# Splitting the first batch pair of a hybrid block into two units, and moving token weighting and softplus sums from VectorE to GpSimd

## The chip, the cores and the metric

The kernel runs on one NeuronCore of a Trainium2 chip. TensorE (PE) multiplies matrices into PSUM, VectorE (DVE) and ScalarE (ACT) do elementwise work, GpSimd (POOL) does some elementwise work and issues DMAs, and the queue of SyncE (SP) issues DMAs. Each engine runs its own list of instructions in order, and semaphores order the engines against each other. The metric is the device time of one execution in microseconds (us); lower is better.

## The reference

The input is 8 batches of 256 tokens with 128 features, in fp32. Four residual layers follow each other:

```
x = x + mamba(layernorm(x))     # selective state space, 256 channels, 16 states
x = x + moe(layernorm(x))       # 8 experts, top 2, inner width 352
x = x + gated_attention(layernorm(x))   # relu(scores)**2
x = x + moe(layernorm(x))       # the same expert weights
```

In the first layer each channel i and state n runs a recurrence over the tokens, `new = exp(A[i,n] * d_t) * state + d_t * B_t[n] * h_t`, and its output sums `new * C_t[n]` over the 16 states and adds `D * h_t`. Here `d = softplus(ts @ dt_w + dt_b)`, and `h` is a causal convolution of width 4 followed by silu. The expert layer gives every token a weight for each expert (zero outside its two best) and adds `w_e * ((x @ w_up) * silu(x @ w_gate)) @ w_down` over the experts.

## The kernel before, in words

The eight batches are four groups of two (`SIZES`, L133), so a group is 512 tokens, and most tiles are 128 features by 512 tokens. Five kinds of work exist for a group g:

- `prelude(g)` (lane s, L518): layer norm, projection, convolution (by DVE for groups 0 and 3, by PE for groups 1 and 2, `CONV`), then B, C and the softplus. B and C go to DRAM as `bc`. The softplus is `max(z,0) + ln(1 + exp(-|z|))` with a correction for the rounding of `1 + exp`. Its four elementwise steps, L622 (the correction), L624 (`dl -= ex`), L632 (`dl += ww`) and L633 (`du = dl * h`), are DVE instructions.
- `recurrence(g)` (lane m, L724): sixteen steps, one for each pair of a chunk of states and a half of the channels. A step is three DVE instructions on a 128x1024 tile `st`: L744 (`st = bt * du`), the scan L749, and L753 (`st *= ct`). A lane of its own (`feeder`, L666) has SP load `bt` and `ct`, broadcast from DRAM, and has ACT make `decay` by exponentials (L697). A tile holds `CHUNK // GB` = 2 states of 512 tokens. Another lane (`adder`, L709) sums the `st` tiles over the chunks by accumulating DMAs on POOL's queue (L716).
- `gating(g)` (lane g) and `ending(g)` (lane f): for groups 0 and 1 PE sums what is left of the states with the identity as weights (tile `y`); the product with the gate is L797 or L784.
- `tail(g)` (lane t): the projection back (`pb_m`), added to the residual x by L512.
- `rest(g)` (lane r): expert layer `p`, attention `a`, expert layer `r`, then the store. An expert layer is `led_in` (norm, router, ranks, weights `we`) and `moe` (22 blocks of gate `gp`, ScalarE's silu `sg`, up `up`, DVE's product `it` at L1000, and down `dn`). The up product of an expert takes tokens already multiplied by their weight: `wb` is loaded by a broadcast DMA on ACT's queue (L969) and multiplied by `xT` on DVE (`weighted`, L974, L977). For the layers in `SOON` the product of expert 0 is made in `led_in` (L940).

All groups run interleaved. The order on every engine is fixed when the program is built, by a planner (`Board`, L32): each lane offers its next operation with an estimated duration, the planner computes when it could start from what it believes of the engines, buffers and inputs, takes the engine that could start first, and among the lanes ready there within a lane's patience the one of lowest rank (`RANKS`). A switch of ScalarE's function table adds 1.3 us to an estimate (`SWITCH`). Where the planner sees PE idle ahead of a product, it fills the time with products of the identity into the same bank (`fill` in `pe`, L320 to L327); in the profile these stand under L325, with two records for each fp32 product. They compute nothing.

The estimates are written beside each operation: `dve_us(512)` is 0.69 us, and the planner knows nothing of one engine slowing another.

Of the kernel before, what the change touches and what calls it, by code (L numbers as in the profile page):

```python
# [31 lines left out]
class Board:  # L32
# [4 lines left out]
    PATIENCE, LONG = 0, 0  # L37
# [58 lines left out]
def kernel(  # L96
# [28 lines left out]
    P = 128  # L125
# [25 lines left out]
        "s": [0, 4, 4, 1.5], "m": [1.5, 2, 3, 3.5],  # L151
        "g": [4, 0, 3.5, 2], "t": [0, 3.5, 3.5, 0.5],
        "r": [2, 0.5, 2.5, 0.5], "f": [2.5, 1.5, 4, 0.5], "w": [0, 0, 0.3, 0], "feeder": 5, "adder": 0,
    }
    SOON = ("p0", "p1", "r0", "p3", "r3")
    SPLIT = ()
# [125 lines left out]
    def ring(pool, shape, tag, name, bufs=1):  # L282

        held = rings.setdefault((pool.name, tag), [])
        free = held[-bufs].used if len(held) >= bufs else 0.0
        h = Held(pool.tile(shape, FP, tag=tag, name=name, bufs=bufs), free)
        held.append(h)
        return h
# [51 lines left out]

    def mm(n):
        return 0.005 + 0.00167 * n
# [37 lines left out]
    ]  # L380
    xh = [
# [4 lines left out]
    padding = [Held(t) for t in padded]  # L386
# [131 lines left out]
    def prelude(g):  # L518

        GB = SIZES[g]  # L520
        G = GB * T
        xn = yield from layernorm(Held(xs[g]), f"m{g}", "m", rms=True, parts=xh[g])
        for held in xh[g]:
            yield from biased(held, b_first)
        xT = ring(norm, [P, G], "xTm", f"xT_m{g}")
        yield from transposed(xn, f"m{g}", xT, scale=col("norm_scale"))
# [3 lines left out]
        h = [ring(mam, [P, G], f"h{c}", f"h_{g}_{c}", bufs=2) for c in range(NI)]  # L530
        cv = ring(mam, [P, NI, GB, T], "ex", f"cv_{g}")
        for c in range(NI):
            hp = padding[c]
            ps = bank([P, G], f"hid_{g}_{c}")
            yield pe(mm(G), [ps], [xT], product(ps.ap, [(in_w_sb[:, c * P : (c + 1) * P], xT.ap)]))
            yield act(act_us(G), [hp], [ps], lambda: nc.scalar.activation(
                hp.ap[:, 0:GB, K - 1 :], ps.ap.rearrange("p (b t) -> p b t", b=GB),
# [4 lines left out]
            if g in CONV:  # L542
                cps = bank([P, GB, T], f"conv_{g}_{c}")
                yield pe(K * mm(G), [cps], [hp], product(
                    cps.ap, [(taps_sb[:, k, c, :], hp.ap[:, 0:GB, k : k + T]) for k in range(K)]
                ))
                yield act(act_us(G), [h[c]], [cps], lambda: nc.scalar.activation(
                    h[c].ap.rearrange("p (b t) -> p b t", b=GB), cps.ap, AF.Silu,
                    bias=col("conv_b", c),
                ), SILU)  # L550
                shut(cps)
                continue

            if g > 0:
                yield act(act_us(G), [cv], [hp], lambda: nc.scalar.mul(
                    cv.ap[:, c], hp.ap[:, 0:GB, 0:T], col("conv_w", c)
                ))

            def taps():
                if g == 0:  # L560
                    nc.vector.tensor_scalar_mul(cv.ap[:, c], hp.ap[:, 0:GB, 0:T], col("conv_w", c))
                for k in range(1, K):
                    nc.vector.scalar_tensor_tensor(
                        cv.ap[:, c], hp.ap[:, 0:GB, k : k + T], col("conv_w", k * NI + c),
                        cv.ap[:, c], ALU.mult, ALU.add,
                    )

            yield dve((K - (g > 0)) * dve_us(G), [cv], [hp], taps)
        for c in range(0 if g in CONV else NI):
            yield act(act_us(G), [h[c]], [cv], lambda: nc.scalar.activation(  # L570
                h[c].ap, cv.ap[:, c].rearrange("p b t -> p (b t)"), AF.Silu, bias=col("conv_b", c)
# [3 lines left out]
        ps = bank([P, G], f"xpj_{g}")  # L575
# [4 lines left out]
        ww = ring(mam, [P, NI, G], "ww", f"ww_{g}")  # L580
# [3 lines left out]
        bc = Held(dram.tile([2 * N, G], FP, tag="bc", name=f"bc_{g}"))  # L584
# [4 lines left out]
        dl = [ring(mam, [P, G], f"dl{c}", f"dl_{g}_{c}", bufs=2) for c in range(NI)]  # L589
        ex = ring(mam, [P, NI, G], "ex", f"ex_{g}")  # L590
        for c in range(NI):
            ps = bank([P, G], f"dt_{g}_{c}")
# [19 lines left out]
        du = [ring(mam, [P, G], f"du{c}", f"du_{g}_{c}", bufs=2) for c in range(NI)]  # L612
# [6 lines left out]
        for (a, b), e, w in zip(parts, exs, wws):  # L619

            def lost():
                nc.vector.scalar_tensor_tensor(e.ap, w.ap, 1.0, e.ap, ALU.subtract, ALU.subtract)  # L622
                for c in range(a, b):
                    nc.vector.tensor_sub(dl[c].ap, dl[c].ap, e.ap[:, c - a, :])  # L624

            yield dve(2 * (b - a) * dve_us(G), [e] + dl[a:b], [w], lost)
        for (a, b), w in zip(parts, wws):
            yield act(act_us((b - a) * G), [w], [], lambda: nc.scalar.activation(w.ap, w.ap, AF.Ln, bias=zero), EXP)
        for (a, b), w in zip(parts, wws):
            for c in range(a, b):  # L630
                def step():
                    nc.vector.tensor_add(dl[c].ap, dl[c].ap, w.ap[:, c - a, :])  # L632
                    nc.vector.tensor_mul(du[c].ap, dl[c].ap, h[c].ap)  # L633

                yield dve(2 * dve_us(G), [dl[c], du[c]], [w, h[c]], step)
# [6 lines left out]
        led_up[g] = bc, h, xT, dl, du  # L642

    def gating(g):

        xT = led_up[g][2]
        G = SIZES[g] * T
        gate = [ring(mam, [P, G], f"g{c}", f"g_{g}_{c}") for c in range(NI)]
        for c in range(NI):
            ps = bank([P, G], f"gat_{g}_{c}")  # L650
# [6 lines left out]
        gates[g] = gate  # L657
# [8 lines left out]
    def feeder():  # L666

        for g in range(NG):
            while f"s{g}" not in done:
                yield None  # L670
            GB = SIZES[g]
            G = GB * T
            NC = CHUNK // GB
            bc, h, _, delta, du = led_up[g]
            for q in range(N // NC):
# [4 lines left out]
                for tag, r0 in (("bt", q * NC), ("ct", N + q * NC)):  # L680
                    t = ring(scan, [P, NC, G], tag, f"{tag}_{g}_{q}", bufs=2)
# [5 lines left out]
                fed[g, q] = *rows_at, das  # L687
                for c in range(NI):
# [15 lines left out]
                    yield act(0.81 * NC, [da], [delta[c]], issue, EXP)  # L704
# [4 lines left out]
    def adder():  # L709

        while len(done & {f"f{g}" for g in range(NG)}) < NG:
# [3 lines left out]
            g, us, acc, st, into, of = sums.pop(0)  # L715
# [4 lines left out]
            landed[g] = landed.get(g, 0) + 1  # L720
# [3 lines left out]
    def recurrence(g):  # L724
        GB = SIZES[g]
# [3 lines left out]
        bc, h, _, delta, du = led_up[g]  # L729
# [4 lines left out]
        for q in range(NQ):  # L734
            for c in range(NI):
                while not spare():
                    yield None
                st = state([P, NC, G], f"st_{g}_{q}_{c}")
                if q == 0:
                    acc.append(st)  # L740
                while len(fed.get((g, q), [[]])[-1]) <= c:
                    yield None
                bt, ct, das = fed[g, q]
# [13 lines left out]
                elif q > 0:  # L757
                    sums.append((g, 6.3, acc[c], st, acc[c].ap, st.ap))
                    count[c] += 1
                elif g > 0:  # L760

                    sums.append((g, 4.5, acc[c], h[c], acc[c].ap[:, 0, :], h[c].ap))
                    count[c] += 1
        recurred[g] = acc, last, sum(count)
# [5 lines left out]
    def ending(g):  # L770

        G = SIZES[g] * T
        NC = CHUNK // SIZES[g]
        acc, last, count = recurred.pop(g)
        bc, h, _, delta, du = led_up[g]
        if g in FOLD:
            for c in range(NI):
                sums.append((g, 4.5, acc[c], acc[c], acc[c].ap[:, 0, :], acc[c].ap[:, 1, :]))
                count += 1
        while landed.get(g, 0) < count or g not in gates:  # L780
            yield None
        for c in range(NI):
            if g in FOLD:
                yield dve(dve_us(G), [du[c]], [gates[g][c], acc[c]], lambda: nc.vector.tensor_mul(  # L784
                    du[c].ap, acc[c].ap[:, 0, :], gates[g][c].ap
# [3 lines left out]
            y = bank([P, G], f"y_{g}_{c}")  # L789
# [7 lines left out]
            yield dve(dve_us(G), [du[c]], [gates[g][c], y], lambda: nc.vector.tensor_mul(  # L797
                du[c].ap, y.ap, gates[g][c].ap
# [3 lines left out]
    def tail(g):  # L802
        gates.pop(g)
        bc, h, _, delta, du = led_up.pop(g)
        G = SIZES[g] * T
        yield from forked((RANKS["t"][g], g), [
            project_back(
                xh[g][p], of_part(g, p, du), out_w_sb, f"m{g}{p}"
            ) for p in range(len(PARTS[g]))
        ])  # L810
# [134 lines left out]
    def moe(g, which, key, shared, ends):  # L945
# [28 lines left out]
        def weighted(e):  # L974

            wb = wx[e]
# [334 lines left out]
```

## Time and profile before

| What | Value |
|---|---|
| Median of 3 runs | 759.33 us (759.11 to 759.85) |
| The profiled execution: its time / its span | 758.34 us / 756.6 us |
| PE busy | 737.7 us (98%) |
| DVE busy | 568.6 us (75%) |
| ACT busy | 431.1 us (57%) |
| POOL busy | 89.8 us (12%) |
| Scans (L749), count and mean | 64, 2309 ns |
| Products `wb * xT` (L977), count | 59 |
| Accumulating DMAs on POOL's queue (L716) | 64 |

The span runs from the first instruction's start to the last one's end; the time of the execution has 1.74 us around it. A busy PE is not a PE that does useful work here, since the filling products count as busy.

### The profile page before, as it was taken

The numbers are of one execution on the slowest core, as the hardware profiler recorded it, in microseconds if no ns is written. First come the engines' busy times: TensorE is split into PE (matmuls) and PEld (weight loads), VectorE is DVE, ScalarE is ACT, GpSimd is POOL, SyncE is SP. The second block draws the span as 40 slices with busy tenths as digits, with TensorE's granted clock in tenths as the row PEclk, the third lists the DMA queues.
The fourth block names the chain that finished last, engine by engine and source line by source line (L and its number), as shares of the span: only waits on it lengthen the run. The fifth ranks groups of instructions, "written<-read, shape, count | busy, mean of one in ns | idle before, by whom it ended". The sixth has DMA issues, their size and how long they took to land.

```text
span 756.6 us, 8464 instructions
## 1 busy us (share of the span) xinstructions
PE 737.7 (98%) x3093; PEld 403.6 (53%) x3093; DVE 568.6 (75%) x824; ACT 431.1 (57%) x570; POOL 89.8 (12%) x110
## 2 busy tenths in 40 slices
PE   4999999999999999999999999999999999999997
PEld 3877996853446744434754533443555434644343
DVE  2599999999999999899999998995735334354332
ACT  5578333799947879977876677742252322432220
POOL 2021110311112210002120110011100001000000
PEclk9999999999999999999999999999999999999999
DMA  8719795399763345655774666745011200000110
GB/s 260 209 57 220 169 219 162 98 228 218 166 171 84 76 124 133 166 133 138 176 170 96 159 161 179 160 102 109 2 42 27 72 15 14 15 29 29 47 36 14
DMA packets 38903, 88.63 MB, mean 117 GB/s; under 512 B 4339, under 2 KB 14542, under 8 KB 38862
## 3 DMA queue, kind: packets, MB, share of 16 engines
q0 software_dynamic: 9312, 30.94, 22.8%
q1 hardware_dynamic: 20624, 41.54, 17.2%
q10 hardware_dynamic: 8926, 15.61, 6.8%
q8 instruction: 24, 0.39, 0.2%
q14 instruction: 17, 0.14, 0.0%
HBM read 55.71 MB, written 1.44 MB: 76 GB/s over the span
## 4 chain that ended last, share of the span: by engine, by line
PE 78%; DVE 15%; ACT 3%; issue 2%; ACTq 0%; DVEq 0%
PE gp_r L487 10%; PE dn_r L1006 10%; PE dn_p L1006 9%; PE gp_p L487 9%; PE up_r L986 7%; PE up_p L986 7%; DVE st L749 6%; PE up_r L993 3%; DVE st L744 3%; PE up_p L993 3%; DVE st L753 2%; PE av_a L1197 2%; PE tp_p L325 1%; PE xpj L325 1%; PE v_a L1131 1%
## 5 line engine op out<-in xcount | busy, mean ns | idle before, releaser
L749 DVE TENSOR_TENSOR_SCAN st<-decay,st 128x1024 f32<-128x1024 f32 x64 | 147.8, 2309 | 2.5
L960 ACT ACTIVATE sg_r<-gp_r,zero 128x512 f32<-128x512 f32 x88 | 59.9, 687 | 109.8 <-PE gp_r L487 88.7
L57 ACT ACT_TABLE_LOAD x89 | 114.2, 1283 | 8.0 <-PE dn_r L1006 3.6
L697 ACT ACTIVATE decay<-dl,zero,a_sb 128x510 f32<-128x510 f32 x128 | 96.2, 804 | 36.9 <-DVE st L749 35.7
L1000 DVE TENSOR_TENSOR it_r<-up_r,sg_r 128x512 f32<-128x512 f32 x88 | 60.4, 687 | 66.7 <-PE up_r L986 42.3
L960 ACT ACTIVATE sg_p<-gp_p,zero 128x512 f32<-128x512 f32 x88 | 59.3, 685 | 62.5 <-PE gp_p L487 46.6
L1000 DVE TENSOR_TENSOR it_p<-up_p,sg_p 128x512 f32<-128x512 f32 x88 | 60.3, 686 | 43.4 <-PE up_p L986 29.4
L1006 PE MATMUL dn_p<-it_p,wd_sb 128*128 128x512 f32 x176 | 91.2, 605 | 0.6 <-DVE it_p L1000 0.6
L1006 PE MATMUL dn_r<-it_r,wd_sb 128*128 128x512 f32 x176 | 90.5, 603 | 0.0
L716 POOL DMA_DIRECT2D st<-st x58 | 50.4, 874 | 334.2 <-DVE st L753 303.7
L487 PE MATMUL gp_r<-xT_r,wg_sb 128*128 128x512 f32 x176 | 90.0, 597 | 0.0
L487 PE MATMUL gp_p<-xT_p,wg_sb 128*128 128x512 f32 x176 | 89.0, 594 | 0.0
L744 DVE TENSOR_TENSOR st<-bt,du 128x1024 f32<-128x1024 f32 x64 | 78.8, 1231 | 0.0
L753 DVE TENSOR_TENSOR st<-st,ct 128x1024 f32<-128x1024 f32 x64 | 78.1, 1221 | 0.7
L986 PE MATMUL up_p<-wb_p,wu_sb 128*128 128x512 f32 x128 | 65.1, 594 | 0.0
L986 PE MATMUL up_r<-wb_r,wu_sb 128*128 128x512 f32 x128 | 64.9, 592 | 0.0
L1006 PEld LDWEIGHTS dn_p<-it_p,wd_sb 128*128 128x128 f32 x176 | 31.3, 189 | 47.1 <-issue 36.3
L487 PEld LDWEIGHTS gp_r<-xT_r,wg_sb 128*128 128x128 f32 x176 | 32.6, 190 | 42.7 <-issue 37.4
L1006 PEld LDWEIGHTS dn_r<-it_r,wd_sb 128*128 128x128 f32 x176 | 31.6, 190 | 44.3 <-issue 39.5
L487 PEld LDWEIGHTS gp_p<-xT_p,wg_sb 128*128 128x128 f32 x176 | 32.8, 190 | 41.2 <-issue 36.3
L325 PEld LDWEIGHTS y<-ident 128*128 128x128 f32 x428 | 48.0, 192 | 1.2 <-PE dt L487 0.8
L325 PE MATMUL y<-ident 128*128 128x128 f32 x428 | 48.2, 275 | 0.0
(217 smaller groups left out, 853.1 us busy)
## 6 DMA issues: line engine op xcount, KB each, us to landing
st<-st POOLq DMA_DIRECT2D x54, 512.0 KB, 6.4
bt<-bc SPq DMA_DIRECT2D x32, 512.0 KB, 6.0
ct<-bc SPq DMA_DIRECT2D x32, 512.0 KB, 4.5
wb_r<-wrow_r ACTq DMA_DIRECT2D x30, 256.0 KB, 3.8
wb_p<-wrow_p ACTq DMA_DIRECT2D x29, 256.0 KB, 3.9
st<-h POOLq DMA_DIRECT2D x6, 256.0 KB, 4.9
wg_sb<-in_L_ffn_w_gate_dram SPq DMA_DIRECT2D x2, 704.0 KB, 4.7
wu_sb<-in_L_ffn_w_up_dram SPq DMA_DIRECT2D x2, 704.0 KB
```

What stands on the lines that cost most here:

```text
L57: self.load_tables(op.table)
L325: nc.tensor.matmul(ps[:, 0:n], lhsT=ident[:, 0:m], rhs=ident[:, 0:n], start=True, stop=True)
L487: nc.tensor.matmul(ps, lhsT=lhsT, rhs=rhs, start=(i == 0), stop=(i == len(terms) - 1))
L697: nc.scalar.activation(shaped[:, n, :, 1:], delta[c].ap.rearrange("p (b t) -> p b t", b=GB)[:, :, 1:], AF.Exp, bias=zero, scale=a_sb[:, c, ...
L716: yield load(us, [acc], [st], lambda: nc.gpsimd.dma_start(into, of, accum_op=ALU.add), "POOL", 0.9)
L744: yield dve(1.22, [st], [bt, du[c]], lambda: nc.vector.tensor_mul(st.ap, bt.ap, du[c].ap.unsqueeze(1).to_broadcast([P, NC, G])))
L749: yield dve(2.29, [st], [das[c]], lambda: nc.vector.tensor_tensor_scan(flat, das[c].ap.rearrange("p n t -> p (n t)"), flat, 0.0, ALU.mult, ...
L753: yield dve(1.22, [st], [ct], lambda: nc.vector.tensor_mul(st.ap, st.ap, ct.ap))
L960: yield act(act_us(G), [sg], [gp], lambda: nc.scalar.activation(sg.ap, gp.ap, AF.Silu, bias=zero), SILU)
L986: nc.tensor.matmul(ps.ap, lhsT=wu_sb[:, i * P : (i + 1) * P], rhs=wa.ap[:, cols_of], start=True, stop=True,)
L1000: yield dve(dve_us(width), [it], [ps, sg], lambda: nc.vector.tensor_mul(it.ap, ps.ap, sg.ap[:, cols_of]))
L1006: yield pe(mm(dn.ap.shape[1]), [dn], [it], lambda: nc.tensor.matmul(dn.ap, lhsT=wd_sb[:, i, :], rhs=it.ap[:, cols_of], start=(i == 0), sto ...
```

## The change

The change does four things.

1. `SPLIT = (0,)`: the two batches of group 0 become units of their own for everything up to the first expert layer. `UNITS` is now a list of five (group, first batch, last batch), and prelude, gating, recurrence, ending and tail take a unit. The two units share tiles of the group's size (`room`), each using its 256 columns. A recurrence chunk of such a unit has `CHUNK // 1` = 4 states of 256 tokens, so a unit has eight steps and the group still has sixteen, on tiles of the same 128x1024. `led_in` of the first expert layer runs for each unit as soon as its tail is done (`come`); after both, the group is one part again and `moe` runs on 512 tokens as before.
2. For the layers `p0`, `r0`, `p1`, `r1` and `p2`, `weighted` issues the product `wb * xT` on POOL (the program has 37 of them there, and 22 are left on DVE).
3. For groups 1 to 3 the softplus' `dl -= ex` and `dl += ww` go to POOL: four instructions of 128x512 in each group, twelve in all. Group 0 keeps them on DVE.
4. The planner's ranks are other ones, the second unit's prelude has a rank made worse by 1.5, and `LONG` is 0.2 instead of 0. The order on every engine changes with that.

```diff
-    PATIENCE, LONG = 0, 0
+    PATIENCE, LONG = 0, 0.2
...
-        "s": [0, 4, 4, 1.5], "m": [1.5, 2, 3, 3.5],
-        "g": [4, 0, 3.5, 2], "t": [0, 3.5, 3.5, 0.5],
-        "r": [2, 0.5, 2.5, 0.5], "f": [2.5, 1.5, 4, 0.5], "w": [0, 0, 0.3, 0], "feeder": 5, "adder": 0,
+        "s": [1.5, 2, 4, 0.5], "m": [1.5, 2, 3, 2.5],
+        "g": [4, 3.5, 2.5, 0.5], "t": [0, 3.5, 1, 3.5],
+        "r": [2, 0.5, 1, 0.5], "f": [2.5, 0, 3.5, 0.5], "w": [0.6, 0.6, 0.3, 0], "late": 1.5, "feeder": 2.5, "adder": 0,
     }
     SOON = ("p0", "p1", "r0", "p3", "r3")
-    SPLIT = ()
+
+    SPARED = ("p0", "r0", "p1", "r1", "p2")
+    SPLIT = (0,)
...
+    def room(pool, u, tag, name, both=False, bufs=1):
+
+        g, lo, hi = UNITS[u]
+        if (g, tag, name) not in rooms:
+            shape = [P, NI, SIZES[g] * T] if both else [P, SIZES[g] * T]
+            rooms[g, tag, name] = ring(pool, shape, tag, f"{name}_{g}", bufs)
+            rooms[g, tag, name].views = []
+        t = rooms[g, tag, name]
+        ap = t.ap[:, :, lo * T : hi * T] if both else t.ap[:, lo * T : hi * T]
+        h = Held(ap, t.used)
+        t.views.append(h)
+        return h
...
+    def pool_us(n):
+        return 0.1 + 0.0024 * n
...
+    UNITS = [(g, lo, hi) for g in range(NG) for lo, hi in PARTS[g]]
+    UNITS_OF = [[u for u, unit in enumerate(UNITS) if unit[0] == g] for g in range(NG)]
...
-    def prelude(g):
-
-        GB = SIZES[g]
+    def prelude(u):
+
+        g, lo, hi = UNITS[u]
+        GB = hi - lo
...
-                nc.vector.scalar_tensor_tensor(e.ap, w.ap, 1.0, e.ap, ALU.subtract, ALU.subtract)
-                for c in range(a, b):
-                    nc.vector.tensor_sub(dl[c].ap, dl[c].ap, e.ap[:, c - a, :])
-
-            yield dve(2 * (b - a) * dve_us(G), [e] + dl[a:b], [w], lost)
+
+            yield dve(dve_us((b - a) * G), [e], [w], lost)
+            for c in range(a, b):
+                if g > 0:
+                    yield pool(pool_us(G), [dl[c]], [e], lambda: nc.gpsimd.tensor_tensor(
+                        dl[c].ap, dl[c].ap, e.ap[:, c - a, :], ALU.subtract
+                    ))
+                else:
+                    yield dve(dve_us(G), [dl[c]], [e], lambda: nc.vector.tensor_sub(
+                        dl[c].ap, dl[c].ap, e.ap[:, c - a, :]
+                    ))
...
-                def step():
-                    nc.vector.tensor_add(dl[c].ap, dl[c].ap, w.ap[:, c - a, :])
-                    nc.vector.tensor_mul(du[c].ap, dl[c].ap, h[c].ap)
-
-                yield dve(2 * dve_us(G), [dl[c], du[c]], [w, h[c]], step)
+                if g > 0:
+                    yield pool(pool_us(G), [dl[c]], [w], lambda: nc.gpsimd.tensor_tensor(
+                        dl[c].ap, dl[c].ap, w.ap[:, c - a, :], ALU.add
+                    ))
+                else:
+                    yield dve(dve_us(G), [dl[c]], [w], lambda: nc.vector.tensor_add(
+                        dl[c].ap, dl[c].ap, w.ap[:, c - a, :]
+                    ))
+                yield dve(dve_us(G), [du[c]], [dl[c], h[c]], lambda: nc.vector.tensor_mul(
+                    du[c].ap, dl[c].ap, h[c].ap
+                ))
...
-                    yield act(0.81 * NC, [da], [delta[c]], issue, EXP)
+                    yield act((0.35 + 0.0009 * G) * NC, [da], [delta[c]], issue, EXP)
...
         def weighted(e):
 
             wb = wx[e]
+            if nm in SPARED:
+                yield pool(pool_us(G), [wb], [xT], lambda: nc.gpsimd.tensor_tensor(
+                    wb.ap, wb.ap, xT.ap, ALU.mult
+                ))
+                return
             yield dve(dve_us(G), [wb], [xT], lambda: nc.vector.tensor_mul(wb.ap, wb.ap, xT.ap))
...
-        yield from forked((RANKS["r"][g], g), [led_in(g, "p", key, p, first) for p in parts])
+        def come(p):
+            while f"t{UNITS_OF[g][p]}" not in done:
+                yield None
+            yield from led_in(g, "p", key, p, first)
+
+        yield from forked((RANKS["r"][g], g), [come(p) for p in parts])
+        if len(parts) > 1:
+
+            joined = Held(xs[g])
+            joined.ready = max(h.ready for h in xh[g])
+            joined.used = max(h.used for h in xh[g])
+            PARTS[g][:], xh[g][:] = [(0, SIZES[g])], [joined]
...
+    def lane(kind, n, g, work, after):
+
+        late = RANKS["late"] if kind == "s" and n in UNITS_OF[g][1:] else 0
+        waiting.append(Lane((RANKS[kind][g] + late, n), work, after))
...
+    for u, (g, lo, hi) in enumerate(UNITS):
+        prior = [v for v in UNITS_OF[g - 1]] if g > 0 else []
+        older = [v for v in UNITS_OF[g - 2]] if g > 1 else []
+        lane("s", u, g, prelude(u), [f"g{v}" for v in prior] + [f"t{v}" for v in older])
+        lane("m", u, g, recurrence(u), [f"s{u}"] + [f"m{u - 1}"] * (u > 0))
+        lane("g", u, g, gating(u), [f"s{u}"] + [f"t{v}" for v in prior])
+        lane("f", u, g, ending(u), [f"m{u}"])
+        lane("t", u, g, tail(u), [f"f{u}", f"g{u}"] + [f"t{u - 1}"] * (u > 0))
+        if lo == 0:
+            lane("r", g, g, rest(g), [f"t{u}"] + [f"r{g - 2}"] * (g > 1))
```

How the two programs differ in numbers of instructions, read from the programs themselves:

| Instruction | Before | After |
|---|---|---|
| PE: filling products of the identity | 564 | 462 |
| of these, ahead of the first gate product of layer `p0` | 430 | 345 |
| PE: `y` products | 14 of 512 columns | 4 of 512 and 36 of 256 |
| DVE, all | 824 | 812 |
| POOL: elementwise 128x512 products and sums that were on DVE | 0 | 49 |
| POOL: accumulating DMAs | 64 | 60 |
| ACT: `decay` exponentials | 128 of 510 columns | 96 of 510 and 64 of 255 |
| ACT: table loads | 89 | 93 |
| SP: writes of `bc` / loads of `bt` and `ct` | 4 / 64 | 5 / 64 |

## Prediction, made before the changed kernel ran

> **What bounds the kernel now.** I read the page's busy times first, then the engines by stretch of time, then who makes DVE wait, and last the chain of work that ended last. The columns of the second table are stretch, its length, then busy time and instructions of each engine, granted clock, DMA share and GB/s.
>
> ```profile
> PE 737.7 (98%) x3093; PEld 403.6 (53%) x3093; DVE 568.6 (75%) x824; ACT 431.1 (57%) x570; POOL 89.8 (12%) x110
> L325 PE MATMUL y<-ident 128*128 128x128 f32 x428 | 48.2, 275 | 0.0
> ```
>
> ```profile
> 41.00:158.00 117.00, 115.27 (x803) 95.07 (x802) 114.47 (x111) 66.34 (x89) 21.50 (x22) 1.00 0.66 160
> 158.00:511.00 353.00, 351.81 (x1278) 171.74 (x1277) 330.75 (x441) 269.36 (x335) 51.64 (x54) 1.00 0.62 149
> 511.00:530.00 19.00, 19.00 (x60) 7.77 (x59) 10.48 (x14) 4.72 (x7) 2.61 (x3) 1.00 0.52 105
> 530.00:756.60 226.60, 221.47 (x760) 104.38 (x758) 95.33 (x214) 66.88 (x103) 7.62 (x7) 1.00 0.10 29
> ```
>
> ```profile
> DVE it_p L1000 <- PE up_p L986: 7.7, 13, 1.7
> DVE it_r L1000 <- PE up_r L986: 4.2, 6, 1.1
> DVE it_r L1000 <- PE up_r L993: 1.1, 3, 0.7
> DVE x L479 <- PE ot_p L476: 0.8, 1, 0.8
> ```
>
> ```profile
> 130.59 1.72 PE gat L487 x4
> 132.31 6.47 PE tp_p L325 x58
> 158.23 1.72 PE gp_p L487 x4
> ```
>
> The 98% of PE mislead: the L325 groups are filling products. Until 158 us DVE is the bound (114.5 of 117 us) and PE fills. From 158 us, where the first expert layer begins, to the last scan at 511 us both are nearly full, PE 351.8 and DVE 330.8 of 353 us; DVE waits for PE there for 13.8 us (the third fence, that stretch alone). After 530 us PE alone works, through a fixed list. From the chain I take PE's prices: a filling product 6.47 / 29 = 0.223 us (two records each), a 512-column product 1.72 / 2 = 0.86 us; one of 256 columns, half, 0.43.
>
> **The change part by part.**
>
> *PE's own list.* Filling products fall from 564 to 462: 102 x 0.223 = -22.8 us. The sums `y` become 36 x 0.43 + 4 x 0.86 instead of 14 x 0.86: +6.9. The other halved products of group 0 cost what they did (two halves). Sum -15.9: if PE never waits longer than before, the span is 756.6 - 15.9 = 740.7 us. That is a floor, since which fills remain was decided by estimates and not by the chip.
>
> *The start.* The first scan stands at 40.98 us. Before it ACT does the gates between two table loads:
>
> ```profile
> 35.33 1.28 ACT L57 ACT_TABLE_LOAD   x1
> 36.62 1.26 ACT L653 ACTIVATE g<-gat,cols 128x512 f32<-128x512 f32 x2
> 37.91 1.28 ACT L57 ACT_TABLE_LOAD   x1
> 39.20 0.81 ACT L697 ACTIVATE decay<-dl,zero,a_sb 128x510 f32<-128x510 f32 x1
> ```
>
> In the new order four sets of `decay` come before the first gate: -3.9 us, and some 1 us from half-size steps ahead of it; I take -5 (0 if the loads of `bt`, 6.0 us to landing, are late; -8 if the halves save more). Behind it ACT gets four more table loads (4 x 1.28 = 5.1 us) and 64 exponentials of 255 columns for 32 of 510: 64 x 0.5 (between 0.39, a 128-column L373, and 0.80) - 32 x 0.80 = +6.3. ACT is idle for 50 of the 117 us there, so nothing; without that cover 11.4.
>
> *SP and DMA.* One `bc` write more; the 512 KB loads of units 0 and 1 come in pieces of 1 KB instead of 2. Two scans last 9.6 us, a `bt` load 6.0, so nothing; at twice 6.0 it would be 2.4 us for each of 8 chunks, 19 us. Four accumulating DMAs go (POOL -3.5 us, off the path).
>
> *DVE, relieved.* 37 products at (21.3 + 19.8) / 59 = 0.697 us are 25.8, 12 sums at 0.69 are 8.2; 37 instructions more for the halves, at some 0.15 (two of 256 columns at 0.415 against one at 0.69), give back 5.5. Net -28.5 us, nearly all before the last scan.
>
> *DVE, held up.* The trace has POOL products of the same 128x512 size, the bias sums L494 (alone 1.27 us). Where DVE works on two tiles in SBUF meanwhile, it stretches:
>
> ```profile
> 45.15 1.66 POOL L494 TENSOR_TENSOR x<-x,b_first 128x512 f32<-128x512 f32 x1 [3.39 <-ACT xn_m L437]
> 45.77 3.18 DVE L749 TENSOR_TENSOR_SCAN st<-decay,st 128x1024 f32<-128x1024 f32 x1
> 357.85 0.69 DVE L1000 TENSOR_TENSOR it_r<-up_r,sg_r 128x512 f32<-128x512 f32 x1
> 358.03 1.39 POOL L494 TENSOR_TENSOR x<-x,b_back 128x512 f32<-128x512 f32 x1
> 358.45 1.53 DVE L977 TENSOR_TENSOR wb_r<-wb_r,xT_r 128x512 f32<-128x512 f32 x1
> 639.57 1.27 POOL L494 TENSOR_TENSOR x<-x,b_back 128x512 f32<-128x512 f32 x1 [1.92 <-DVE xn_a L422]
> 640.28 0.69 DVE L1000 TENSOR_TENSOR it_r<-up_r,sg_r 128x512 f32<-128x512 f32 x1 [0.79 <-PE up_r L986]
> ```
>
> The scan takes 3.18 for 2.31 (+0.87), the L977 1.53 for 0.69 (+0.84); three more such meetings cost 0.77 (an L744 at 144.1 us, 1.99 for 1.22), 0.45 (a scan at 241.1, 2.76) and 0.99 (an L899 at 253.5, 1.41 for 0.42). L1000, which reads PSUM, stays at 0.69 (last line). So a moved instruction costs DVE between 0 and 0.99 us. All 49 but three are due before the last scan. I take 0.55: in the expert layers every second DVE instruction is an L1000, and the one meeting where a PSUM-reading instruction (an L512) ran first is the 0.45. 46 x 0.55 = +25.3, against -28.5. Bounds 0 and 45.5.
>
> The Trainium skill, "SBUF — State Buffer", section "SBUF: two separate sides", speaks against the change: the port pair that VectorE and GpSimd share is held exclusively for a whole instruction, against VectorE instructions with two SBUF inputs, and the loser blocks fully. The stretched rows agree in kind; by size the rule would make each of the 46 cost the whole 1.27 us, 58 us, and the time some 786 us, where the dearest row has 0.99.
>
> *New waits.* POOL's queue is in order. A `wb` product now stands behind accumulating DMAs that wait for a scan, and PE's `up` behind the product; the norms' L415 (1.0 to 1.9 us) stand there too; accumulating DMAs stand behind products that wait for their load (3.8 us to landing). The three free `st` buffers turn over in (4.8 + 0.9 + 6.4) / 3 = 4.0 us against 7.3 us a scan on average, which covers 3 us. `du` (L633) now waits on DVE for POOL's sums; the steps queued behind it are scans. Bounds: 0, and 3 groups x 2.5 us (two POOL sums) = 7.5. I set this against the 13.8 us that DVE waits for PE and that an earlier PE frees: of these I count 7.
>
> *The sum.* Last scan: 510.7 - 5 - 28.5 + 25.3 - 7 = 495.5. From the last scan to the last `pb_m` on PE lie 18.7 us (529.4 - 510.7: accumulation, fold, product), unchanged. Behind it PE had 227.2 us; in the new order 9.1 us more stand there (205 products of 512 columns instead of 194, one up block in pieces more, six fills fewer): 236.3. Span 495.5 + 18.7 + 236.3 = 750.5, above the floor of 740.7. The profiled execution has 1.74 us around its span, and the median lay 1.0 above it: 753.3, I say 753.5.
>
> **The rivals.**
>
> 1. *The port makes DVE the bound: slower.* For: the mean of the five meetings is 0.78, and the nearest in place (358 us, an expert layer) is 0.84. Against: much of DVE's work there reads PSUM. With 0.78 the last scan is at 506.1 and the time 763.8; with 0.99, 773.4. It decides from 0.68 on, where the last scan reaches 501.6 and the span 756.6 again.
> 2. *PE's list rules: much faster.* If a moved instruction costs DVE 0.3 or less, the last scan falls to 484 and PE to its floor: 740.7 + 2.7 = 743.5. For: PE lists 85 fills fewer before the first expert layer, which could begin at 143 us. Against: five of five meetings at a busy DVE cost 0.45 or more.
> 3. *The split buys nothing.* If ACT's table loads or the 1 KB pieces hold the first scans up, the 5 us go and the time is 758.5: within 0.2%.
>
> **How the numbers follow.** A measurement tells 0.2%, 1.5 us, from no change. Forecast (747 to 757.8): 0.40. Rival 2 (under 747): 0.11. Rival 3 and other cases within 757.8 to 760.9: 0.10. Rival 1: 0.39, a tenth of all beyond 770. Faster 0.51, same 0.10, slower 0.39. The range 743 to 770 leaves out some 0.13; the forecast's own is 747 to 757.8.
>
> **What would show it.** First scan before 38 us; first `gp_p` between 140 and 148; `wb` products on POOL of 1.3 to 3.5 us, with scans near 3 us beside them, and DVE's busy time up by about 0.5 us for each; last scan at 490 to 500, last `pb_m` 18 to 20 us behind. I am wrong if scans lengthen by 0.8 for each product, if PE waits for `wb`, or if POOL's accumulating DMAs come late enough that scans wait for `st`.

## The result, and the profile after

The changed kernel takes 763.94 us (median of 4 runs, 763.11 to 765.49) against 759.49 us for the kernel before in the runs beside it (759.11 to 759.85). The ratio is 1.0061, with a 95% interval of 1.0042 to 1.0080: slower, by more than the 0.2% that a measurement can tell. The forecast was 753.5 us and faster. The time lies in the range of 743 to 770, and it is that of rival 1 (763.8 us).

The profiled execution took 763.11 us, with a span of 761.3 us. From the page, busy times and the three instructions of a recurrence step (`st = bt * du`, the scan, `st *= ct`; columns: busy us, mean ns of one):

```profile
span 761.3 us, 8302 instructions
PE 729.3 (96%) x2957; PEld 396.9 (52%) x2957; DVE 579.4 (76%) x812; ACT 449.5 (59%) x624; POOL 173.6 (23%) x158
L796 DVE TENSOR_TENSOR_SCAN st<-decay,st 128x1024 f32<-128x1024 f32 x64 | 156.7, 2448 | 3.4 <-ACT decay L743 0.7
L791 DVE TENSOR_TENSOR st<-bt,du 128x1024 f32<-128x1024 f32 x64 | 92.6, 1447 | 0.0
L800 DVE TENSOR_TENSOR st<-st,ct 128x1024 f32<-128x1024 f32 x64 | 82.2, 1285 | 0.4
```

DVE has 12 instructions less than before and is busy 10.8 us longer (568.6 before). The work that stayed got slower. The same three groups before, where the product ahead of the scan is L744 and the one behind it L753:

```profile
L749 DVE TENSOR_TENSOR_SCAN st<-decay,st 128x1024 f32<-128x1024 f32 x64 | 147.8, 2309 | 2.5
L744 DVE TENSOR_TENSOR st<-bt,du 128x1024 f32<-128x1024 f32 x64 | 78.8, 1231 | 0.0
L753 DVE TENSOR_TENSOR st<-st,ct 128x1024 f32<-128x1024 f32 x64 | 78.1, 1221 | 0.7
```

The stages, in the columns of the second fence of the prediction (granted clock, DMA share and GB/s last):

```profile
158.00:511.00 353.00, 340.91 (x1185) 161.98 (x1187) 338.67 (x395) 264.79 (x328) 118.28 (x95) 0.99 0.63 150
511.00:530.00 19.00, 19.00 (x68) 8.81 (x61) 9.62 (x15) 4.81 (x7) 5.50 (x5) 1.00 0.44 97
530.00:761.30 231.30, 227.22 (x762) 104.95 (x760) 98.29 (x215) 68.88 (x106) 9.25 (x8) 1.00 0.09 28
```

In the expert stretch DVE does 395 instructions instead of 441 and is busy 338.7 us instead of 330.8; PE is busy 10.9 us less. DVE's waits in that stretch, which before began with 7.7, 4.2 and 1.1 us for the up products of PE:

```profile
DVE du L845 <- PE y L515: 1.4, 2, 1.1
DVE xn_r L450 <- POOL rstd_r L443: 0.9, 1, 0.9
DVE xn_p L450 <- POOL rstd_p L443: 0.9, 1, 0.9
...
DVE it_p L1049 <- PE up_p L1035: 0.8, 1, 0.8
DVE it_r L1049 <- PE up_r L1035: 0.7, 3, 0.4
```

DVE hardly waits for PE any more (1.5 us for the up products there). It is the bound. Where the time goes is seen in the timeline of one step (start in us, duration in us), first DVE's:

```profile
172.96 1.22 DVE L800 TENSOR_TENSOR st<-st,ct 128x1024 f32<-128x1024 f32 x1
174.09 0.68 DVE L1049 TENSOR_TENSOR it_p<-up_p,sg_p 128x512 f32<-128x512 f32 x1
174.69 3.03 DVE L791 TENSOR_TENSOR st<-bt,du 128x1024 f32<-128x1024 f32 x1
177.83 2.29 DVE L796 TENSOR_TENSOR_SCAN st<-decay,st 128x1024 f32<-128x1024 f32 x1
```

and POOL's at the same time:

```profile
174.48 0.86 POOL L762 DMA_DIRECT2D st<-st  x1 [4.96 <-DVE st L800]
175.04 1.60 POOL L1022 TENSOR_TENSOR wb_p<-wb_p,xT_p 128x512 f32<-128x512 f32 x1
```

The end of L800 releases an accumulating DMA on POOL's queue, and the moved product stands directly behind it. So the product begins 0.86 us after L800's end (174.18). In that time DVE has done one L1049, and the product meets the next instruction, an L791 with two inputs in SBUF. That one takes 3.03 us; the shortest L791 takes 1.21 and the median 1.22.

The norm's L450 is held too, although it reads only one tile (and two columns of one value for each partition). Four of them that together take 1.12 us when the products are made tiny (the first experiment) take 4.20 beside two products in a row:

```profile
270.79 4.20 DVE L450 TENSOR_SCALAR xn_r<-x,mv_r,rstd_r 128x128 f32<-128x128 f32 x4 [0.94 <-POOL rstd_r L443]
271.38 2.76 POOL L1022 TENSOR_TENSOR wb_p<-wb_p,xT_p 128x512 f32<-128x512 f32 x2
```

### The profile page after: what moved, and what is told of

Same layout as the page of the kernel before. It is cut to its first block, busy times and chain, and to the rows that moved or that the text cites. A ratio compares the mean times of both kernels' runs of the same rounds, so it can differ in the third digit from the quotient of the medians.

```text
span 761.3 us, 8302 instructions
## 1 busy us (share of the span) xinstructions
PE 729.3 (96%) x2957; PEld 396.9 (52%) x2957; DVE 579.4 (76%) x812; ACT 449.5 (59%) x624; POOL 173.6 (23%) x158
## 4 chain that ended last, share of the span: by engine, by line
PE 64%; DVE 22%; issue 6%; ACT 3%; POOL 2%; DMA 2%; ACTq 0%; DVEq 0%; POOLq 0%
PE dn_r L1055 10%; PE gp_r L515 9%; PE dn_p L1055 7%; PE up_r L1035 7%; PE gp_p L515 7%; DVE st L796 6%; DVE st L791 5%; PE up_p L1035 5%; DVE st L800 4%; PE up_r L1042 3%; PE up_p L1042 2%; PE av_a L1246 2%; DVE it_p L1049 2%; PE v_a L1180 1%; PE conv L515 1%
## 5 line engine op out<-in xcount | busy, mean ns | idle before, releaser
L796 DVE TENSOR_TENSOR_SCAN st<-decay,st 128x1024 f32<-128x1024 f32 x64 | 156.7, 2448 | 3.4 <-ACT decay L743 0.7
L743 ACT ACTIVATE decay<-dl,zero,a_sb 128x510 f32<-128x510 f32 (+1 forms) x160 | 104.7, 717 | 11.2 <-DVE st L796 10.7
L1049 DVE TENSOR_TENSOR it_r<-up_r,sg_r 128x512 f32<-128x512 f32 x88 | 59.7, 685 | 63.0 <-PE up_r L1035 38.1
L762 POOL DMA_DIRECT2D st<-st x54 | 47.5, 890 | 256.9 <-DVE st L800 219.1
L791 DVE TENSOR_TENSOR st<-bt,du 128x1024 f32<-128x1024 f32 x64 | 92.6, 1447 | 0.0
L1049 DVE TENSOR_TENSOR it_p<-up_p,sg_p 128x512 f32<-128x512 f32 x88 | 59.6, 681 | 36.0 <-PE up_p L1035 24.7
L800 DVE TENSOR_TENSOR st<-st,ct 128x1024 f32<-128x1024 f32 x64 | 82.2, 1285 | 0.4
L345 PEld LDWEIGHTS tp_m<-ident 128*128 128x128 f32 x418 | 47.1, 192 | 1.0 <-issue 0.5
L345 PE MATMUL tp_m<-ident 128*128 128x128 f32 x418 | 47.2, 275 | 0.0
```

Of the source, the lines that this page charges most:

```text
L345: nc.tensor.matmul(ps[:, 0:n], lhsT=ident[:, 0:m], rhs=ident[:, 0:n], start=True, stop=True)
L743: nc.scalar.activation(shaped[:, n, :, 1:], delta[c].ap.rearrange("p (b t) -> p b t", b=GB)[:, :, 1:], AF.Exp, bias=zero, scale=a_sb[:, c, ...
L762: yield load(us, [acc], [st], lambda: nc.gpsimd.dma_start(into, of, accum_op=ALU.add), "POOL", 0.9)
L791: yield dve(1.22, [st], [bt, du[c]], lambda: nc.vector.tensor_mul(st.ap, bt.ap, du[c].ap.unsqueeze(1).to_broadcast([P, NC, G])))
L796: yield dve(2.29, [st], [das[c]], lambda: nc.vector.tensor_tensor_scan(flat, das[c].ap.rearrange("p n t -> p (n t)"), flat, 0.0, ALU.mult, ...
L800: yield dve(1.22, [st], [ct], lambda: nc.vector.tensor_mul(st.ap, st.ap, ct.ap))
```

## The experiments

Three explanations were open: POOL's products hold DVE up (the shared port of rival 1); the waits on POOL's queue do; or the split and the order that the planner made with it are worth nothing, or less. The planner fixes every order from its own estimates, so the experiments of the first kind leave its estimates alone and change only the instruction that an operation issues. The order of everything else then stays what it was.

### The product made tiny, in the changed order

```diff
-                yield pool(pool_us(G), [wb], [xT], lambda: nc.gpsimd.tensor_tensor(
-                    wb.ap, wb.ap, xT.ap, ALU.mult
-                ))
+                yield pool(pool_us(G), [wb], [xT], lambda: nc.gpsimd.memset(wb.ap[:, 0:1], 0.0))
```

> The changed kernel in its own order, with the 37 products that it has on POOL replaced by a POOL instruction that writes one column of the same tile (the tokens' weighting is left out for these experts). POOL's queue and every wait for it stay, the work on 512 columns goes. Theory 1 (the held port: each POOL instruction of 128x512 costs DVE some 0.8 us): DVE loses 37 x 0.8 = 30 us of busy time, its rows L791, L796 and L800 fall back towards 1.23, 2.31 and 1.22 us, the last scan comes 18 to 30 us before 510 us, and PE's list rules, 743 to 749 us. Theory 2 (POOL's queue: products and accumulating DMAs stand behind each other in order, and PE or DVE waits): all those waits are still there, 757 to 763 us. Theory 3 (the split and the new order themselves lose the time): 757 to 764 us too, but with DVE's busy time lower and DVE waiting for PE.

Measured: 747.22 us (745.15 to 749.75), ratio to before 0.984 (0.9817 to 0.9863). From the page:

```profile
PE 725.5 (97%) x2957; PEld 396.8 (53%) x2957; DVE 549.1 (74%) x812; ACT 448.4 (60%) x624; POOL 117.1 (16%) x158
L796 DVE TENSOR_TENSOR_SCAN st<-decay,st 128x1024 f32<-128x1024 f32 x64 | 147.8, 2309 | 3.7 <-ACT decay L743 1.1
L791 DVE TENSOR_TENSOR st<-bt,du 128x1024 f32<-128x1024 f32 x64 | 80.1, 1252 | 0.0
```

and DVE's waits from 158 to 511 us:

```profile
DVE it_p L1047 <- PE up_p L1033: 13.1, 13, 1.9
DVE it_r L1047 <- PE up_r L1033: 2.9, 8, 0.9
DVE it_r L1047 <- PE up_r L1040: 2.5, 7, 1.1
DVE it_p L1047 <- PE up_p L1040: 2.4, 2, 2.1
```

Every instruction of DVE, every place in POOL's queue and every semaphore is still there; only POOL's reading and multiplying is gone (so the tokens of these experts are not weighted). DVE does the same 812 instructions in 30.3 us less, and the scan is back at 2309 ns. So a product on POOL held DVE for 30.3 / 37 = 0.82 us on average. With DVE relieved the waits for PE are back (20.9 us in the four lines).

### The product back on DVE, in the changed order

```diff
-                yield pool(pool_us(G), [wb], [xT], lambda: nc.gpsimd.tensor_tensor(
+                yield pool(pool_us(G), [wb], [xT], lambda: nc.vector.tensor_mul(
-                    wb.ap, wb.ap, xT.ap, ALU.mult
+                    wb.ap, wb.ap, xT.ap
                 ))
```

> The changed kernel in its own order, the 37 products issued at the same place but on DVE; the 12 softplus sums stay on POOL. Theory 1: DVE gets rid of 37 x 0.8 = 30 us of being held and pays 37 x 0.66 = 24 us for the products: last scan some 6 us earlier, 756 to 761 us. Theory 2: the waits in POOL's queue go, and PE's products come when DVE's order says: 748 to 755 us. Theory 3: no change, 762 to 766 us.

Measured: 751.44 us (749.16 to 752.87), ratio 0.9892 (0.9872 to 0.9911). From the page:

```profile
span 749.2 us, 8270 instructions
PE 726.2 (97%) x2957; PEld 395.9 (53%) x2957; DVE 568.6 (76%) x849; ACT 448.8 (60%) x624; POOL 115.7 (15%) x121
L791 DVE TENSOR_TENSOR st<-bt,du 128x1024 f32<-128x1024 f32 x64 | 79.4, 1240 | 0.0
```

and a stretch of DVE's timeline:

```profile
177.49 0.67 DVE L1049 TENSOR_TENSOR it_p<-up_p,sg_p 128x512 f32<-128x512 f32 x1
178.07 0.68 DVE L1022 TENSOR_TENSOR wb_p<-wb_p,xT_p 128x512 f32<-128x512 f32 x1
178.67 1.22 DVE L800 TENSOR_TENSOR st<-st,ct 128x1024 f32<-128x1024 f32 x1
```

37 more instructions on DVE make it 10.8 us less busy than the changed kernel. Against the kernel with the tiny product they cost (568.6 - 549.1) / 37 = 0.53 us each: a row shows 0.68, but the next instruction starts 0.60 after it (178.07 to 178.67), because neighbours overlap. So the product costs DVE 0.53 us when DVE does it and 0.82 us when POOL does it. This kernel is 1.6% faster than the changed one and 1.1% faster than before.

The time lies in the range expected for theory 2 (POOL's queue), not in that of theory 1, which counted 0.66 us for a product on DVE. The stages decide between them: the last scan comes 14.0 us earlier (496.1 instead of 510.1 us), and of these 12.6 are DVE's work up to there (458.1 instead of 470.6 us) and only 1.4 its idle time (38.0 instead of 39.5). So the queue had little part in it. Nor did the clock: two runs here at a granted clock of 0.993 took 751.9 and 752.9 us, two of the changed kernel at 0.992 took 763.1 and 763.3.

### The product on POOL, in the order of before

```diff
+            if nm in ("p0", "r0", "p1", "r1", "p2"):
+                yield dve(dve_us(G), [wb], [xT], lambda: nc.gpsimd.tensor_tensor(
+                    wb.ap, wb.ap, xT.ap, ALU.mult
+                ))
+                return
             yield dve(dve_us(G), [wb], [xT], lambda: nc.vector.tensor_mul(wb.ap, wb.ap, xT.ap))
```

> The kernel before in its own order, with the products of the same five layers (p0, r0, p1, r1, p2) issued on POOL at the same place; no split, softplus on DVE. Theory 1: DVE saves 37 x 0.66 = 24 us and is held 37 x 0.8 = 30 us, of which its 13.8 us of waiting for PE take some up: 758 to 766 us, DVE busy time up by 5 us or so. Theory 2: POOL's queue was made by no plan here, so products come late: 765 to 785 us, with PE waiting for wb. A port that costs little (0.3): DVE waits more for PE, same time as before, 757 to 760 us.

Measured: 766.31 us (765.93 to 768.72), ratio 1.0088 (1.0072 to 1.0105). From the page:

```profile
PE 743.7 (97%) x3093; PEld 405.3 (53%) x3093; DVE 584.7 (76%) x787; ACT 431.8 (56%) x570; POOL 143.9 (19%) x147
L749 DVE TENSOR_TENSOR_SCAN st<-decay,st 128x1024 f32<-128x1024 f32 x64 | 156.3, 2442 | 2.5
L744 DVE TENSOR_TENSOR st<-bt,du 128x1024 f32<-128x1024 f32 x64 | 103.9, 1623 | 0.0
```

The same move slows the old order too, and not by POOL's queue: from 143 to 525 us no wait of PE for `wb` is recorded. DVE is busy 16.1 us longer (some 5 were expected) with 37 instructions less; with 0.53 us a product from the run above that makes (16.1 + 37 x 0.53) / 37 = 0.97 us held per product, an estimate, since the 0.53 is from the other order. The hold depends on what the product meets: here L744, which has two SBUF inputs, takes most of it (1623 for 1231 ns).

### All 49 moved instructions back on DVE

The edit above, and the two sums of the softplus as well:

```diff
-                    yield pool(pool_us(G), [dl[c]], [e], lambda: nc.gpsimd.tensor_tensor(
-                        dl[c].ap, dl[c].ap, e.ap[:, c - a, :], ALU.subtract
+                    yield pool(pool_us(G), [dl[c]], [e], lambda: nc.vector.tensor_sub(
+                        dl[c].ap, dl[c].ap, e.ap[:, c - a, :]
...
-                    yield pool(pool_us(G), [dl[c]], [w], lambda: nc.gpsimd.tensor_tensor(
-                        dl[c].ap, dl[c].ap, w.ap[:, c - a, :], ALU.add
+                    yield pool(pool_us(G), [dl[c]], [w], lambda: nc.vector.tensor_add(
+                        dl[c].ap, dl[c].ap, w.ap[:, c - a, :]
```

> The changed kernel in its own order, all 49 instructions (37 products, 12 softplus sums) issued at the same place but on DVE: the split and the new order alone. Theory 1 (the held port): with the 37 products on DVE the time was 751.4 us; each of the 12 sums then still held DVE some 0.8 us and would cost 0.53 to 0.69 on DVE: 1.5 to 3.5 us less, 747 to 751 us, and the scans' mean at 2290 to 2300 ns. Rival (the sums on POOL are a gain, since they run beside scans and shorten the way from the softplus to the first product du): 753 to 757 us.

Measured: 751.62 us (749.42 to 752.27), ratio 0.9887 (0.9866 to 0.9908); DVE 569.5 us busy, last scan at 496.1 us as in the run before. The time lies between the two expected ranges: twelve sums on POOL or on DVE make no difference that shows. What is left here of the change is the split and its order, and that is worth 1.1%. So the change has two parts of opposite sign: -1.1% for the split and its order, +1.6% for the products on POOL.

### The split alone, planned anew

```diff
-    SPARED = ("p0", "r0", "p1", "r1", "p2")
+    SPARED = ()
...
-                if g > 0:
+                if False:
```

> The changed kernel with the split and its ranks, but with nothing moved to POOL; the planner makes a new order (574 filling products). Theory 1: the split alone is a little dearer on PE (6.9 us more of y, 10 fills more, 2.2 us) and starts 5 us earlier: 757 to 767 us. Theory 3 (the split is what costs): 768 us or more. If the split is a gain that POOL spoils: 745 to 754 us.

Measured: 772.28 us (769.59 to 772.5), ratio 1.0161 (1.0143 to 1.0178), which by the expectation would mean that the split costs time. The run above has the same work on the same engines, but for the fills (462, here 574), and takes 20.7 us less, so the split need not cost that. The difference is the order that the planner makes when it is told that DVE has this work. DVE is busy about as long (572.5 us) but idle for 32.4 us between 158 us and the last scan, for 13.8 in the run above. From DVE's waits from 36 to 524 us:

```profile
DVE it_p L1049 <- PE up_p L1035: 7.5, 13, 1.3
DVE du L845 <- PE y L515: 6.1, 3, 4.2
DVE it_r L1049 <- PE up_r L1035: 4.4, 7, 1.6
```

### No split, all on DVE

The run with all 49 on DVE, with this:

```diff
-    SPLIT = (0,)
+    SPLIT = ()
```

> The changed kernel's planner, ranks and estimates, so an order made as if 37 products and 12 sums were POOL's, but without the split, and all 49 run on DVE. With the split the same gave 751.6 us. If the split is the gain (first expert layer some 10 us earlier): without it 758 to 764 us. If the gain is the new ranks and the planner's optimism about DVE: 748 to 755 us.

Measured: 775.01 us (773.02 to 777.1), ratio 1.0196 (1.0176 to 1.0217): far above what was expected. The first scan comes at 41.8 us instead of 34.5, the first gate product at 149.1 instead of 140.3, and DVE is idle for 28.9 us between 158 us and the last scan. With the ranks of the changed kernel, and an order planned for each, the kernel with the split is 23 us faster. But without the split and with its own ranks the kernel before takes 759.5 us: ranks and split belong together, and no single run prices the split by itself. Why the planner's orders of this run and of the one before are 15 to 20 us worse was not traced further and stays open.

### POOL only writes

```diff
-                yield pool(pool_us(G), [wb], [xT], lambda: nc.gpsimd.tensor_tensor(
-                    wb.ap, wb.ap, xT.ap, ALU.mult
-                ))
+                yield pool(pool_us(G), [wb], [xT], lambda: nc.gpsimd.memset(wb.ap, 0.0))
```

> The changed kernel in its own order, the 37 products on POOL replaced by a POOL memset of the same 512 columns: POOL writes the tile and reads nothing (the weighting is left out for these experts). If what holds DVE is POOL's reading of SBUF, this goes like the run that wrote one column: 745 to 750 us, the rows of st at 1.24, 2.31 and 1.24 us. If any POOL instruction of this size holds DVE for its length, the rows stretch by the memset's own length each, 750 to 760 us, according to how long it takes.

Measured: 751.35 us (746.28 to 754.55), ratio 0.9884 (0.9832 to 0.9936). From the page:

```profile
L1022 POOL MEMSET wb_p<- 128x512 f32 x22 | 14.3, 684 | 6.1 <-DMA wb_p<-wrow_p 6.1
L791 DVE TENSOR_TENSOR st<-bt,du 128x1024 f32<-128x1024 f32 x64 | 79.4, 1240 | 0.0
```

DVE is busy 551.1 us, 2.0 more than with the tiny product: 0.05 us for each on average. The three instructions of the recurrence are not held by POOL's writing (the mean L791 takes 1240 ns, 1252 with the tiny product). The norm's L450 is, at the same place as above, now beside two memsets:

```profile
269.16 2.50 DVE L450 TENSOR_SCALAR xn_r<-x,mv_r,rstd_r 128x128 f32<-128x128 f32 x4 [0.94 <-POOL rstd_r L443]
269.73 1.28 POOL L1022 MEMSET wb_p<- 128x512 f32 x2
```

That is 1.4 of the 2.0 us. The times spread as the granted clock does: the two runs at 746.3 and 748.2 us had 0.997, the two at 754.5 had 0.986. In the profiled one it falls to 0.59 between 240 and 250 us, where PE is busy for 10.00 of the 10 us. So the busy time of DVE, and not the median, is what this run tells.

### POOL reads one tile

```diff
-                yield pool(pool_us(G), [wb], [xT], lambda: nc.gpsimd.tensor_tensor(
-                    wb.ap, wb.ap, xT.ap, ALU.mult
+                yield pool(pool_us(G), [wb], [xT], lambda: nc.gpsimd.tensor_scalar(
+                    wb.ap, wb.ap, 0.5, None, ALU.mult
                 ))
```

> The changed kernel in its own order, the 37 products on POOL replaced by a POOL product of the tile with a constant: one tile in SBUF is read instead of two (the weighting is left out for these experts). If DVE is held for the length of a POOL instruction that reads SBUF, the cost is in proportion to its length: at 0.4 to 0.7 us instead of 1.27, 750 to 757 us. If it needs two read tiles on POOL's side, as DVE's: 745 to 750 us.

Measured: 751.76 us (749.42 to 755.99), ratio 0.9911 (0.988 to 0.9942). From the page:

```profile
L1022 POOL TENSOR_SCALAR wb_p<-wb_p 128x512 f32<-128x512 f32 x22 | 41.8, 1930 | 4.8 <-DMA wb_p<-wrow_p 3.4 <-PE up_p L1035 1.0 <-PE gp_r L515 0.3
L791 DVE TENSOR_TENSOR st<-bt,du 128x1024 f32<-128x1024 f32 x64 | 84.0, 1312 | 0.0
```

DVE is busy 559.5 us: (559.5 - 549.1) / 37 = 0.28 us held per instruction. The instruction is longer than the product (1.93 for 1.65 us on average) and holds DVE a third as much. (The expectation had put its length at 0.4 to 0.7 us; the time falls in one of its ranges with that premise wrong.) So the hold does not follow POOL's length. It grows with the tiles that POOL reads from SBUF: none 0.05, one 0.28, two 0.82 us. The three are different instructions, though, so that reading alone makes the difference is argued and not shown.

### Fewer filling products

On the kernel with all on DVE (117 fills fewer) and on the kernel before (134 fewer), no fills from the first gate product on:

```diff
+    begun = False
...
-            for _ in range(int((idle - 0.3) / self.FILL)):
+            for _ in range(0 if self.begun else int((idle - 0.3) / self.FILL)):
...
+            Board.begun = True
```

> The order with the split and all 49 on DVE (751.6 us), without the 117 filling products that stand behind the first gate product (117 x 0.223 = 26 us of PE's list); nothing that is computed is left out. If the fills stand in the way of products that could have run: 727 to 745 us. If they only fill time in which PE waits for DVE, whose last scan at 496 us sets the end: 748 to 753 us. If PE's clock falls when it idles, as between 120 and 130 us in the changed kernel (0.83): slower, 753 to 762 us.

> The kernel before in its own order without the 134 filling products behind the first gate product (30 us of PE's list); nothing that is computed is left out. DVE's last scan at 511 us and 18.7 + 227 us behind it set the end if the fills only fill waits: 753 to 759 us. If they stand in the way: 730 to 750 us. If the clock falls with idling: 760 to 768 us.

Measured: 753.6 us (749.37 to 755.76), ratio 0.9916 (0.9883 to 0.9949), for the first, where 751.62 had all its fills; and 762.53 us (761.71 to 764.65), ratio 1.0045 (1.0031 to 1.0059), for the second. The stages of the first (granted clock third from the end):

```profile
143.00:158.00 15.00, 11.26 (x28) 4.07 (x27) 13.90 (x20) 13.87 (x19) 5.45 (x4) 0.77 0.74 181
158.00:511.00 353.00, 334.58 (x1033) 148.06 (x1032) 332.57 (x440) 264.05 (x328) 57.16 (x57) 0.97 0.64 151
```

With the fills these stretches had a clock of 1.00. So the fills behind the first gate product stand in nobody's way: without them PE idles more and its clock is lower, and the kernel is no faster, the old one slower by 0.45%.

## Why the prediction was wrong

The sign is wrong by one term of the sum above all: what POOL's products hold up (18.7 us forecast for the 37, 30.3 measured). What their leaving relieves was also too large (25.8 us, 19.5 measured), and every other term was off by less than 5 us.

*PE's own list.* 102 fills fewer were booked as -22.8 us, in a floor of 740.7 us. It is a floor and nothing more: taking 134 fills from the kernel before made it slower. The sum did not rest on it.

*The start.* First scan at 35.84 us (forecast about 36), first gate product at 142.9 (140 to 148). Right, also that ACT's extra table loads and the 1 KB pieces cost nothing there. What was missed lies behind it: DVE's idle time from the first scan to 158 us grew from 2.5 to 6.0 us (1.2 us of it for the norms' `rstd` and 1.1 for a softplus sum, both from POOL), and PE waited once, 3.7 us, for the states that the first sums `y` read.

*DVE, relieved.* 37 products were booked at the 0.697 us of their rows. DVE gained 0.53 for each, 19.5 us instead of 25.8, since in a full queue the rows overlap. The instructions for the halves were booked at +5.5; with all 49 back on DVE its busy time is 569.5 us against 568.6 before, so they cost 0.9. The two errors nearly cancel.

*DVE, held up.* This is the step that failed. It took 0.55 us for each instruction on POOL, and argued that every second DVE instruction of the expert layers reads PSUM and goes free. Half of that holds: L1049 lasts 681 and 685 ns on average, as before, and none of them takes more than 0.69 us. But they are not every second instruction. Between 158 and 511 us before, in the columns of the groups above:

```profile
L1000 DVE TENSOR_TENSOR it_p<-up_p,sg_p 128x512 f32<-128x512 f32 x55 | 37.6, 683 | 8.5 <-PE up_p L986 7.7 <-issue 0.5
L1000 DVE TENSOR_TENSOR it_r<-up_r,sg_r 128x512 f32<-128x512 f32 x44 | 30.1, 684 | 5.5 <-PE up_r L986 4.2 <-PE up_r L993 1.1
```

That is 99 of 441 instructions and 67.7 of 330.8 us, a fifth; the three instructions of the recurrence take 201.2 us there (98.8 + 51.2 + 51.2). So a product mostly finds DVE on an instruction with two tiles in SBUF, and the trace gave little ground to take 0.78, the mean of its meetings, down to 0.55. The measured average is 0.82 us. Nor do the products fall evenly over DVE's list: 27 of the 37 stand directly behind an accumulating DMA, and 17 of these begin 0.86 to 0.92 us after the end of an L800, where an L791 or a scan often runs or comes next. How much of the 0.82 this makes was not tried by itself. Of the 30.3 us, 24.3 stand in the three instructions of the recurrence (156.7 + 92.6 + 82.2 = 331.5 us; with the tiny product 147.8 + 80.1 + 79.3 = 307.2), and 3.9 in the norm's L450 of layers r (8.3 and 4.4 us). Rival 1 with 0.78 us gave 763.8. Its mechanism is the one measured; that the number fits to 0.2 us is partly luck: its last scan, at 506.1 us, is 4.0 too early, and what lies behind the last scan was 3.8 shorter than the 255.0 us forecast.

The terms of DVE's work together, as changes of its busy time:

| | Forecast | Measured |
|---|---|---|
| 37 products leave DVE | -25.8 | -19.5 |
| DVE held up by them | +18.7 (34 x 0.55) | +30.3 |
| 12 sums, relieved and held | -1.6 | -0.9 |
| instructions for the halves | +5.5 | +0.9 |
| sum | -3.2 | +10.8 |

*Waits.* 7 us were counted as recovered from the waits for PE. From 158 us to the last scan DVE's idle time fell from 22.3 to 14.3 us, 7.9 less. The size is right. With all 49 on DVE it is 13.8, so this gain belongs to the order and not to the move. The queue of POOL, feared in the prediction, cost little: PE waited 0.6 us for `wb`, DVE 0.9 twice for a norm's L443 and 1.1 for the softplus' sums.

*The sum.* The last scan came at 510.1 us instead of 495.5. Of the 14.6 us, DVE's work up to there is 11.3 (busy 470.6 us; 462.5 before, and 3.2 less was forecast) and its idle time 3.3 (39.5 us; 48.2 before, and 12 less was forecast). The last group's `pb_m` began 16.6 us behind (at 526.65 us; 18.7 forecast, also to the first of its products), and 234.7 us lay behind that (236.3): 510.06 + 16.59 + 234.66 = 761.3. With the products on DVE the same stages are 496.1 + 18.2 + 234.9 = 749.2. That this is near the forecast 750.5 is a chance of the errors: the forecast was not made for that kernel.

*Rival 2* had a price too low: with nothing held at all (the tiny product) the last scan is at 492.5 us and not at 484, because DVE waits for PE by then (the 20.9 us). *Rival 3* is out: the 5 us at the start are there.

*The port.* The Trainium skill, "SBUF — State Buffer", section "SBUF: two separate sides", lets the pair of ports be held for the whole of an instruction where VectorE's has two SBUF inputs and POOL's reads SBUF, or where VectorE's runs in a 2-port perf mode (a faster mode that takes the shared pair as well). The runs agree on the first case: L1049, with one input in PSUM, is never stretched, and beside a POOL instruction that only writes the recurrence is not. L450, with one tile and held even beside memsets (2.50 for 1.12 us), may be the second case; no row shows an instruction's mode. At one meeting the whole instruction is about right as well: the L791 of the timeline is 3.03 - 1.22 = 1.81 us longer beside a product of 1.60. As a price for each of the moved instructions it was too dear (58 us for 46; 30.3 were measured for 37), since not every product meets such an instruction. The one-tile instruction, held 0.28 us at 1.93 us of length, fits the rule less well.

## What to carry to other kernels

Elementwise work with two inputs in SBUF is not free on GpSimd while VectorE is the bound and works on SBUF itself: here a product cost VectorE 0.82 us there and 0.53 us at home. To estimate such a move, take the price from the meetings that the old trace has (0.78 here), and before taking anything off it, count by time what VectorE runs in that stretch and what stands on it when the event that starts the GpSimd instruction comes. And to price one part of a change under a planner, keep the order and swap the instruction alone: the same work planned anew was 20.7 us slower.

## What was not expected of the hardware

A product of 1.27 us (alone) can cost another engine more than its own length, while it is itself longer: 1.81 us at the L791 shown, beside a product of 1.60, and 1.84 at the worst L791; POOL's own products last 1.65 and 1.82 us on average. Whether the DMA that POOL issues just ahead has a part in it was not tried by itself; with the tiny product the same DMAs are there and L791 takes 1252 ns on average, 12 more than with the product on DVE.

Behind short waits of PE its clock falls. Two stretches of the changed kernel, with waits of PE of 3.7 and 3.2 us in them:

```profile
120.00:130.00 10.00, 6.30 (x25) 5.03 (x24) 7.98 (x7) 5.37 (x8) 3.03 (x2) 0.83 0.15 58
...
270.00:280.00 10.00, 6.83 (x27) 4.21 (x26) 8.77 (x10) 5.60 (x8) 4.13 (x4) 0.83 0.45 105
```

The clock of 0.83 over 10 us is worth 1.7 us of full speed beside the wait. The second wait is for the L450 that the two products held, and its dip is not there with the product on DVE (1.00 between 270 and 280 us); the first is. A third dip (0.83 between 324 and 334 us) stands behind a wait of 2.4 us. The Trainium skill, "TensorE: Matmul & The Clock Gate", section "What's actually happening", puts the fall behind at least one idle window of about 3.4 us. Only the first of the three waits is that long, and in the kernel with memsets the clock was 0.59 over 10 us in which PE was busy throughout. So a wait of that length is not the whole condition here; what else is was not tried.
